# Graph attention with a residual norm: queries without an edge, their mean row, and two batches' halves in one tile

## The chip, the cores and the metric

The kernel runs on one core of a Trainium2 chip. The metric is the device time of one execution in microseconds (us). Five engines run side by side, each in the order of its own instructions: PE (matrix products), DVE (vector), ACT (scalar activations), POOL (which also issues all indirect DMAs) and SP (which issues plain DMAs). They wait for each other on semaphores.

## The reference

Inputs are x (16 batches of 1024 rows of 512), an adjacency matrix adj of 1024 x 1024 zeros and ones that all batches share, and four 512 x 512 weights with biases; all float32. There are 8 heads of 64.

```python
q = (x @ Wq + bq).reshape(b, n, H, HD)      # k and v alike
scores = jnp.einsum('bqhd,bkhd->bhqk', q, k) / jnp.sqrt(jnp.float32(HD))
scores = scores + (1.0 - adj)[None, None, :, :] * -1000000000.0
attn = jax.nn.softmax(scores, axis=-1)
out = jnp.einsum('bhqk,bkhd->bqhd', attn, v).reshape(b, n, d)
x = _layernorm(x + out @ Wo + bo, axis=-1)
```

The graph is sparse: of the 1024 queries 60 have no edge and 141 have one; the largest number is 66. A query without an edge has -1e9 added to every score. In float32 the scores vanish beside 1e9, all weights are equal, and its attention is the mean of all v. So every query without an edge of one batch has the same row of attention, and the same row after Wo. Only x differs from query to query.

## The kernel before

**Order by degree.** At the start the kernel sorts the queries by their number of edges (`ranks`, L404) and writes the sorted list to `order` in DRAM. A tile is 128 queries of like degree; there are NT = 8 per batch. `asked_row` holds the query numbers of each tile, and x, y and the output rows are gathered and stored by it, with indirect DMAs on POOL. `key_row` holds, for each tile and slot, the row of the key that each query attends to. Tile 0 holds the 64 lowest ranks (those without an edge, and here four with one) and ranks 192 to 255 (up to two edges). Tile 1 (ONE_KEY) holds ranks 64 to 191, which have one edge: their attention is just the v row of their key.

**Blocks.** A block is one slot of one tile: 128 queries, each with one key. `blocks` (L949) lists them over batches, tiles and slots: 34 per batch, 544 in all. `gather` (L958) fetches the k and v rows of a block (`kvg`, 128 rows of 4 KB, one indirect DMA on POOL) eight blocks ahead. DVE multiplies q with k (`products`, L1005) and adds up by head (`scores`, L1009); ACT takes exponentials (L1019); the v row is weighted by ACT in eight pieces (L1029) or by DVE (L1033); DVE adds the slots of one query (L1045). Slots beyond a query's degree carry a row number out of range and -1e9 in `absent`. The highest tiles have further blocks for spread-out edges, whose sums go through PE (L1054, L1055). `normalise` divides, `turn` transposes on PE (poT, L1088).

A query without an edge takes part in two blocks of tile 0: its key is row N of `kv_rows`, which holds zeros for k and the mean of v. `mean_pe` (L708) makes that mean for each batch.

**Fronts.** The other work of PE is the "fronts": x tiles are gathered (L817), transposed (pxT, L606), and multiplied into q (L639, all tiles but ONE_KEY) and into k and v by pairs of tiles (L763, a seven-product scheme). k and v rows of tile t go to DRAM by indirect DMA (L685), into one of ROWS = 3 rings `kv_rows[b % ROWS]`; q tiles go to `q_rows` by SP (L671) and come back by SP as `qt` (L972).

**Finish.** `finish` (L845) multiplies a turned tile with Wo (po, L639), adds x (`y`) and the bias, takes mean and variance (DVE L867, L868; ACT L875; a power on POOL L881), normalises on ACT (L889) and stores the rows with an indirect DMA on POOL (L893). While fronts last, bo_bc is added on DVE; afterwards a bf16 matmul (L940) puts it into the product.

**Spill and stored.** 20 tiles (SPILL) have their turned attention put to DRAM and are finished only after the last front. For the 42 tiles of STORED the front also writes the x tile to `residual`, from which SP loads y later; for all others y is gathered by POOL.

**The order.** Everything is laid out by hand in one loop over steps n, one per block. Each step issues its share of block work, deferred functions (`later`), and then units of fronts or finishes until a credit (`share`, costed by PRODUCT, SUM, TRANSPOSE) is spent. 39 steps of fronts alone lead in. From step (LATE + 1) * NBT on the share is set so that the fronts end 12 blocks before the last batch begins.

**The guard.** The equal weights hold only if |q||k| stays small. `squares` takes the norms of q in tile 0's edgeless rows (L649, sq_q) and of all k rows; `guard` (L1107) checks their product against LIMIT = 31, and if it fails a general path computes everything again.

Of the kernel before, what the change touches and what calls it, by code (L numbers as in the profile page):

```python
# [34 lines left out]
LONE, ONE_KEY, ONE_KEY_AT = 64, 1, (7, 4)  # L35
# [3 lines left out]
SPILL = (*range(36, 100, 4), *range(102, 106))  # L39
STORED = {*SPILL, *range(102, 128)}  # L40
# [14 lines left out]
BIAS_AT = -8  # L55
REST_FROM = {7: -24, 6: -9}
# [113 lines left out]
def kernel(  # L170
# [75 lines left out]
    with ExitStack() as main:  # L246
# [17 lines left out]
        place = one.tile([P, SPAN], F32, name="place")  # L264
# [18 lines left out]
        key_row = one.tile([P, NS + NK], I32, name="key_row")  # L283
        query_row, query_row0 = (one.tile([P, NS], I32, name=name) for name in ("query_row", "query_row0"))

        absent = one.tile([P, NK], F32, name="absent")
        check = one.tile([P, 2 * NT + 2], F32, name="check")

        lone = one.tile([P, 1], F32, name="lone")
        lone_norm = one.tile([P, B], F32, name="lone_norm")  # L290
# [4 lines left out]
        rank_row, asked_row = (one.tile([P, NT], I32, name=name) for name in ("rank_row", "asked_row"))  # L295
# [3 lines left out]
        kv_rows = [dram.tile([N + 1, 2 * D], F32, name=f"kv_rows_{i}") for i in range(ROWS)]  # L299
        q_rows = [dram.tile([N, D], F32, name=f"q_rows_{i}") for i in range(ROWS)]  # L300
        order = dram.tile([N, 2 + TOP], F32, name="order")
        kv_views = [dram_disjoint_views(rows, NT) for rows in kv_rows]
        order_views = dram_disjoint_views(order, NT)
        out_views = dram_disjoint_views(out, B * NT)
# [8 lines left out]
        def loads():  # L313
# [14 lines left out]
            for i in range(ROWS):  # L328
                nc.scalar.dma_start(kv_rows[i][N:N + 1, 0:D], zeros[0:1, 0:D])
                if i:  # L330
                    nc.scalar.dma_start(q_rows[i][ds(ONE_KEY * P, P), :], zeros[:, 0:D])
# [14 lines left out]
        def bias_setup():  # L346
# [6 lines left out]
            nc.vector.tensor_reduce(bk_norm, n4, axis=AX.X, op=OP.max)  # L353
            yield
# [48 lines left out]
        def ranks():  # L403
# [47 lines left out]
            nc.vector.tensor_copy(asked_row, ranked[:, :, 0])  # L451
# [19 lines left out]
            nc.vector.tensor_scalar(absent, absent, -NEG, None, op0=OP.mult)  # L471
# [4 lines left out]
            listed.update(SHORT)  # L476

# [12 lines left out]
        def edges(t):  # L490
# [34 lines left out]
            if J > SEGMENT:  # L525

                nc.vector.tensor_scalar(found[:, 0:J], kl[:, 0:J], 0.0, None, op0=OP.is_gt)
                nc.vector.tensor_reduce(st[:, 0:1], found[:, 0:J], axis=AX.X, op=OP.add)
                nc.vector.tensor_tensor(check[:, 2 * NT + 1:], ranked[:, t, 1:2], st[:, 0:1], op=OP.subtract)
# [56 lines left out]

        X, XT, SX, KV, VSUM, NRM, Y, OT, PS = {}, {}, {}, {}, {}, {}, {}, {}, {}
# [13 lines left out]
        def transpose_x(b, t):  # L601
            def pe():
# [5 lines left out]
                def out():  # L608
                    XT[b, t] = work.tile([P, D], F32, tag="xT", name=f"xT_{b}_{t}", bufs=4)
                    nc.scalar.copy(XT[b, t], p)  # L610
                    n = b * NT + t + 3
                    if b * NT + t in STORED:
# [33 lines left out]
        def squares(name, s, sums, scale=1.0):  # L646
            for h in range(NPAIR):
                sq = work.tile([P, P], F32, tag="sq", name=f"sq_{name}_{h}", bufs=2)
# [7 lines left out]
        def pair(b, j):  # L656
# [8 lines left out]
            def out_q(i, p):  # L665

                assert gathered[0] >= NBT * (b - ROWS + 1)
# [14 lines left out]
            def send(i):  # L682
                kv = KV[b, tt[i]]
                if b:
                    later(2, lambda: nc.gpsimd.indirect_dma_start(  # L685
                        out=kv_views[b % ROWS][tt[i]], out_offset=bass.IndirectOffsetOnAxis(ap=asked_row[:, tt[i]:tt[i] + 1], axis=0),
# [19 lines left out]
            def mean_pe():  # L706
# [3 lines left out]
                def out():  # L710
                    m = work.tile([1, D], F32, tag="q", name=f"mean_{b}", bufs=2)
                    nc.scalar.copy(m, p[0:1, :])  # L712
                    nc.sync.dma_start(kv_rows[b % ROWS][N:N + 1, D:], m)
# [3 lines left out]
                later(1, out)  # L717

# [6 lines left out]
            )  # L725
            n = b * NT + 2 * j + 2
# [94 lines left out]

        def load_y(b, t, k=None):
# [8 lines left out]
            if b * NT + t in STORED:  # L831
                nc.sync.dma_start(Y[b, t], residual[b * NT + t])
            else:
                gather_x(Y[b, t], b, t)
# [7 lines left out]
        def finish(b, t):  # L842


            biased = not fronts and now[0] < total  # L845

            if now[0] >= total:
                nc.vector.tensor_tensor(Y[b, t], Y[b, t], bo_bc, op=OP.add)

            fronts_then = bool(fronts)  # L850

            def out(p):
                OT.pop((b, t))
                y = Y[b, t]

                single = fronts or now[0] > total + 3
                if single:
                    st = small.tile([P, 5], F32, name="stats", bufs=6)
# [449 lines left out]
```

## Time and profile before

| | |
|---|---|
| median of 3 runs | 1929.36 us (1926.79 to 1929.45) |
| the profiled execution | 1928.59 us, of which its span (first to last instruction) is 1926.8 |
| mean granted clock of PE | 0.990 |
| DMA | 550.85 MB, mean 286 GB/s |
| indirect DMAs on POOL | kvg 544, stores 128, kv_rows 120, x 120, qg 96, y 86, v 16, qt 7 |

Busy times are unions of the records of one engine. A record of PE is longer than the pitch at which matmuls follow each other, since they overlap; the chain of waits gives the pitch. In a group of instructions the columns are line, engine and operation, what is written and read, the count, busy us and mean ns of one. In the timeline a bracket holds the idle time before an instruction and what released it.

By stage: until about 130 us the sort and the lead-in; from there 15 batches of about 111 us; the last front unit ends near 1776 us; then the last batch's blocks and 33 finishes, to the end.

### The profile page before, as it was taken

The page shows a single profiled execution, that of the slowest core. Times are in us where ns is not written, and L with a number is a line of the kernel's source. Part 1 is how long each engine was busy: PE and PEld are TensorE (multiplying, and loading weights), DVE is VectorE, ACT ScalarE, POOL GpSimd, SP SyncE. Part 2 cuts the span into 40 slices and gives each one's busy share as a digit, 9 for nine tenths or more (in the row PEclk, how much of TensorE's full clock was granted, in tenths as well). Part 3 has the DMA queues.
Part 4 walks back from the last instruction along what each step waited for, and adds up shares of the span by engine and source line. Part 5 has one row for each costly group of instructions (what it writes and reads, how often), then busy time and mean ns, then how long its engine had stood idle before and what let it go on. Part 6 is the DMA issues. An engine that isn't in the chain of part 4 may idle for free. (4 is left out here: it accounts for less than half of the span.)

```text
span 1926.8 us, 25037 instructions
## 1 busy us (share of the span) xinstructions
PE 1854.1 (96%) x5247; PEld 898.2 (47%) x5247; DVE 1724.8 (90%) x3494; ACT 1549.6 (80%) x6072; POOL 1368.9 (71%) x1262
## 2 busy tenths in 40 slices
PE   7989999999999999999999999999999989899996
PEld 3444454444544454444544454444544444444443
DVE  6888889899998999899998999899998989798885
ACT  3638779878888888889897888888897988788785
POOL 1336667878787777878778788877787777665785
PEclk9999999999999999999999999999999999999998
DMA  7357788888889898898989898988899898888994
GB/s 273 122 179 243 247 276 265 291 273 290 301 273 314 273 305 299 296 315 296 315 267 323 286 326 288 316 294 297 310 316 325 281 334 301 296 287 283 365 328 167
DMA packets 189313, 550.85 MB, mean 286 GB/s; under 512 B 31359, under 2 KB 31371, under 8 KB 189150
## 3 DMA queue, kind: packets, MB, share of 16 engines
q0 software_dynamic: 133584, 447.59, 69.1%
q1 hardware_dynamic: 52672, 96.04, 13.6%
q10 hardware_dynamic: 2894, 5.52, 0.9%
q14 instruction: 119, 0.97, 0.2%
q8 instruction: 44, 0.72, 0.2%
HBM read 426.56 MB, written 147.18 MB: 298 GB/s over the span
## 5 line engine op out<-in xcount | busy, mean ns | idle before, releaser
L1029 ACT ACTIVATE pv<-kvg,pv 128x64 f32<-128x64 f32 x3544 | 892.1, 338 | 0.0
L984 POOL DMA_INDIRECT kvg<-kv_rows,key_row x544 | 624.6, 1148 | 240.8 <-issue 84.8
L639 PE MATMUL pq<-wq,xT 128*128 128x512 f32 x904 | 422.5, 598 | 0.9 <-ACT mean L712 0.9
L639 PE MATMUL po<-wo,oT 128*128 128x512 f32 x864 | 401.2, 597 | 1.0 <-ACT oT L1092 0.9
L1009 DVE TENSOR_REDUCE s<-qk 128x8 f32<-128x512 f32 x544 | 369.5, 679 | 7.5
L1005 DVE TENSOR_TENSOR qk<-qt,kvg 128x512 f32<-128x512 f32 x448 | 306.5, 684 | 37.4 <-DMA kvg<-kv_rows,key_row 37.0
L639 PEld LDWEIGHTS pq<-wq,xT 128*128 128x128 f32 x904 | 169.1, 192 | 193.4 <-issue 179.4
L639 PEld LDWEIGHTS po<-wo,oT 128*128 128x128 f32 x864 | 162.9, 191 | 182.9 <-issue 169.4
L763 PE MATMUL x<-b,xT 128*128 128x512 f32 x504 | 238.1, 595 | 0.0
L763 PE MATMUL pp<-t,s 128*128 128x512 f32 x504 | 237.4, 593 | 0.0
L1045 DVE TENSOR_TENSOR pv<-pv,pv 128x520 f32<-128x520 f32 x336 | 232.7, 692 | 0.9 <-ACT pv L1029 0.9
L1019 ACT ACTIVATE pv<-s,absent 128x8 f32<-128x8 f32 x448 | 130.2, 292 | 84.7 <-DVE s L1009 79.3
L817 POOL DMA_INDIRECT x<-in_x_dram,asked_row x120 | 134.2, 1118 | 76.7 <-PE pxT L606 34.6
L893 POOL DMA_INDIRECT out_dram<-y,asked_row x128 | 146.8, 1147 | 40.8 <-issue 19.3
L685 POOL DMA_INDIRECT kv_rows<-kv,asked_row x120 | 135.9, 1132 | 33.8 <-issue 22.9
L649 ACT ACTIVATE sq_k<-kv 128x128 f32<-128x128 f32 x512 | 150.6, 299 | 7.8 <-DVE kv L786 7.8
L763 PEld LDWEIGHTS x<-b,xT 128*128 128x128 f32 x504 | 95.2, 191 | 114.9 <-issue 109.2
L763 PEld LDWEIGHTS pp<-t,s 128*128 128x128 f32 x504 | 94.3, 190 | 110.6 <-issue 102.6
L954 POOL DMA_INDIRECT qg<-q_rows,query_row x96 | 108.1, 1126 | 31.2 <-issue 25.7
L763 PE MATMUL z<-b,s 128*128 128x512 f32 x252 | 118.8, 594 | 1.0 <-DVE kv L791 0.9
L763 PE MATMUL z<-t,s 128*128 128x512 f32 x252 | 119.6, 597 | 0.0
L763 PE MATMUL pp<-t,xT 128*128 128x512 f32 x252 | 118.4, 592 | 0.0
(208 smaller groups left out, 2666.3 us busy)
## 6 DMA issues: line engine op xcount, KB each, us to landing
q_rows<-q SPq DMA_DIRECT2D x113, 256.0 KB
qt<-q_rows SPq DMA_DIRECT2D x105, 256.0 KB
residual<-x SPq DMA_DIRECT2D x42, 256.0 KB
y<-residual SPq DMA_DIRECT2D x42, 256.0 KB
kvg<-kv_rows,key_row POOLq DMA_INDIRECT x544, 5.9
spill<-oT SPq DMA_DIRECT2D x20, 256.0 KB
oTs<-spill SPq DMA_DIRECT2D x20, 256.0 KB
adj<-in_adj_dram POOLq DMA_DIRECT2D x8, 512.0 KB, 13.4
```

The lines of the kernel that those rows point to most:

```text
L639: nc.tensor.matmul(p, lhs(c), w[:, c, :], start=(c == 0), stop=(c == NPAIR - 1))
L649: nc.scalar.activation(sq, s[:, ts(h, P)], AF.Square, scale=scale, accum_out=sums[:, h:h + 1])
L685: later(2, lambda: nc.gpsimd.indirect_dma_start(out=kv_views[b % ROWS][tt[i]], out_offset=bass.IndirectOffsetOnAxis(ap=asked_row[:, tt[i]: ...
L763: nc.tensor.matmul(R[bank], l[:, ts(c, P)], right[:, c, :], start=(first and c == 0), stop=(c == 1), skip_group_check=True,)
L817: nc.gpsimd.indirect_dma_start(out=y, out_offset=None, in_=x_rows, in_offset=bass.IndirectOffsetOnAxis(ap=asked_row[:, t:t + 1], axis=0), ...
L893: nc.gpsimd.indirect_dma_start(out=out_rows[b, t], out_offset=bass.IndirectOffsetOnAxis(ap=asked_row[:, t:t + 1], axis=0), in_=y, in_offse ...
L984: nc.gpsimd.indirect_dma_start(out=KG[n], out_offset=None, in_=kv_rows[b % ROWS], in_offset=bass.IndirectOffsetOnAxis(ap=key_row[:, g:g + ...
L1005: nc.vector.tensor_tensor(QK[n], q, KG[n][:, 0:D], op=OP.mult)
L1009: nc.vector.tensor_reduce(S[n], QK.pop(n).rearrange("p (h d) -> p h d", d=HD), axis=AX.X, op=OP.add)
L1019: nc.scalar.activation(PV[n][:, D:], S.pop(n), AF.Exp, bias=bias)
L1029: nc.scalar.activation(pv[:, ts(h, HD)], v[:, ds(D + h * HD, HD)], AF.Copy, scale=pv[:, D + h:D + h + 1])
L1045: nc.vector.tensor_tensor(PV[b, t], PV[b, t], pv, op=OP.add)
```

## The change

For batches 2 to 15 (PAIRED_FROM = 2), taken in pairs of an even and an odd batch:

- **The one-edge tile moves down by eight ranks.** It becomes ranks 56 to 183 (column A of a new list `others`), so that its first row is a query without an edge, whose key row is the mean. After Wo its row 0 is the attention output of every edgeless query; `keep_mean` copies it and SP writes it to `mean_rows`.
- **The 56 edgeless queries of two batches form one tile of 112 rows (L).** `load_lone` broadcasts the two mean rows over 56 rows each (SP), gathers y, and four steps later `complete` (the second half of the old `finish`) adds, normalises and stores. It has no q, no blocks, no turn and no Wo product.
- **The two-edge halves (ranks 192 to 255) of two batches form one merged tile 0 (M)** of the odd batch. Its q comes from a product on `BOTH`, into which ACT copies the right halves of both batches' transposed x. Its two kvg gathers are made in halves of 64 rows, one from each batch. The even batch has no tile 0: 32 blocks, no q product, turn or finish.
- **The eight one-edge queries left over per batch (ranks 184 to 191)** have their v rows gathered by two 8-row DMAs per pair into `more_rows`; all 112 form one tile MORE, turned and finished in the last batch.
- **The guard** bounds the q norms of the edgeless queries from a bf16 product of the upper halves of the float32 words (`lone_product`: four matmuls, eight squares per pair), plus a term from the norms of x (sq_x) and Wq.
- kv_rows gets four rings for three; STORED loses tiles 0 and 1 of the last batches (36 tiles for 42); SPILL holds other tiles, 20 as before. In the last batch the one-edge tile is turned earlier (ONE_KEY_LAST).

```diff
-LONE, ONE_KEY, ONE_KEY_AT = 64, 1, (7, 4)
+LONE, ONE_KEY, ONE_KEY_AT, ONE_KEY_LAST = 64, 1, (7, 4), (3, 0)
+PAIRED_FROM, SPARED = 2, 56
+LONE_TILE, MORE_TILE, MORE_AT = 8, 9, (5, 0)
-SPILL = (*range(36, 100, 4), *range(102, 106))
-STORED = {*SPILL, *range(102, 128)}
+SPILL = (*(8 * b + t for b in range(4, 12) for t in (3, 6)), 102, 103, 106, 107)
+STORED = {*SPILL, *(i for i in range(102, 128) if i % 8 > 1)}
...
+        def more_ranks():
+            A, M, L, X = range(4)
+            for col, at, lo, hi in ((A, 0, SPARED, SPARED + P), (M, 0, LONE + P, 2 * P), (M, LONE, LONE + P, 2 * P), (L, 0, 0, SPARED), (L, SPARED, 0, SPARED)):
+                nc.sync.dma_start(others[at:at + hi - lo, col, :], order[lo:hi, :])
+            spare, n = LONE - SPARED, B - PAIRED_FROM
+            lo = SPARED + P
+            for i in range(n):
+                nc.sync.dma_start(others[spare * i:spare * (i + 1), X, :], order[lo:lo + spare, :])
...
+            for h in range(HEADS):
...
+                nc.scalar.activation(sq, W["q"][:, :, ts(h, HD)], AF.Square, accum_out=wq_norm[:, h:h + 1])
...
                     nc.scalar.copy(XT[b, t], p)
+                    if t == 0 and b >= PAIRED_FROM:
+                        if not merged(b):
+                            BOTH[b // 2] = work.tile([P, 2, NPAIR, P], F32, tag="place", name=f"both_{b}", bufs=1)
+                        nc.scalar.copy(
+                            BOTH[b // 2].rearrange("p w c (h n) -> p h c w n", h=2)[:, b % 2],
+                            p.rearrange("p (c w n) -> p c w n", c=NPAIR, w=2),
+                        )
+                        sq = work.tile([P, D], F32, tag="ysq", name=f"sq_x_{b}", bufs=1)
+                        nc.scalar.activation(sq[0:LONE, :], xs[0:LONE, :], AF.Square, accum_out=x_norm[0:LONE, b:b + 1])
...
+                    for c in range(NPAIR):
+                        nc.tensor.matmul(
+                            p, high(both[:, 0, c, :]), high(W["q"][:, c, :]), start=(c == 0), stop=(c == NPAIR - 1)
+                        )
...
+            if j == 0 and b >= PAIRED_FROM:
+                q0 = []
+                if merged(b):
+                    q0 = product(f"pq_{b}_0", lambda c: BOTH[b // 2][:, 1, c, :], W["q"], lambda p: out_q(0, p))
+                    q0 += lone_product()
...
+        def load_lone(b):
+            Y[b, "mean"] = work.tile([P, D], F32, tag="y", name=f"means_{b}", bufs=Y_BUFS)
+            for i in range(2):
+                nc.sync.dma_start(
+                    Y[b, "mean"][SPARED * i:SPARED * (i + 1), :], mean_rows[b - 1 + i:b + i, :].to_broadcast([SPARED, D])
+                )
+            load_y(b, LONE_TILE)
+            later(4, lambda: complete(b, LONE_TILE, Y.pop((b, "mean")), True))
+
+        def keep_mean(b, p):
+            m = work.tile([1, D], F32, tag="q", name=f"out_mean_{b}", bufs=2)
+            nc.scalar.copy(m, p[0:1, :])
+            nc.sync.dma_start(mean_rows[b:b + 1, :], m)
+            if merged(b):
+                later(2, lambda: lone_tiles.append(b))
...
-        blocks = [(b, t, i) for b in range(B) for t in range(NT) if t != ONE_KEY for i in range(OWN[t] + BLOCKS[t])]
+        blocks = [(b, t, i) for b in range(B) for t in tiles_of(b) if t != ONE_KEY for i in range(OWN[t] + BLOCKS[t])]
...
+            if merged(b) and (t, i) == (0, 0):
+                n2, g2 = LONE - SPARED, NS + NK + 3
+                more = work.tile([P, D], F32, tag="qt", name=f"more_{b}", bufs=Q_BUFS)
+                for h in range(2):
+                    nc.gpsimd.indirect_dma_start(
+                        out=more[h * n2:(h + 1) * n2, :], out_offset=None, in_=kv_of(b - 1 + h),
+                        in_offset=bass.IndirectOffsetOnAxis(ap=key_row[0:n2, g2:g2 + 1], axis=0), element_offset=D,
+                    )
...
-            nc.gpsimd.indirect_dma_start(
-                out=KG[n], out_offset=None, in_=kv_rows[b % ROWS],
-                in_offset=bass.IndirectOffsetOnAxis(ap=key_row[:, g:g + 1], axis=0),
-                bounds_check=N, oob_is_err=False,
-            )
+            halves = 1 + (merged(b) and t == 0)
+            for h in range(halves):
+                at = slice(h * P // halves, (h + 1) * P // halves)
+                nc.gpsimd.indirect_dma_start(
+                    out=KG[n][at, :], out_offset=None, in_=kv_of(b + 1 + h - halves),
+                    in_offset=bass.IndirectOffsetOnAxis(ap=key_row[0:P // halves, g:g + 1], axis=0),
+                    bounds_check=N, oob_is_err=False,
+                )
```

## The prediction

> **What bounds the kernel now.** I read part 1 of the page first, then the windows of the middle, the chain that ended last, and the waits and timeline of single engines.
>
> ```profile
> PE 1854.1 (96%) x5247; PEld 898.2 (47%) x5247; DVE 1724.8 (90%) x3494; ACT 1549.6 (80%) x6072; POOL 1368.9 (71%) x1262
> ```
>
> PE leads, and POOL looks as if it had 29% to spare. By windows (columns: PE, PEld, DVE, ACT, POOL busy us, clock, DMA share, GB/s):
>
> ```profile
> 600.00:800.00 200.00, 196.90 (x567) 95.96 (x566) 187.89 (x370) 170.95 (x684) 155.65 (x142) 1.00 0.87 297
> 800.00:1000.00 200.00, 197.56 (x569) 96.25 (x568) 188.44 (x368) 173.83 (x704) 151.74 (x140) 1.00 0.88 298
> 1000.00:1200.00 200.00, 196.35 (x563) 96.83 (x562) 187.76 (x368) 169.05 (x685) 157.25 (x143) 0.99 0.91 307
> 1200.00:1400.00 200.00, 197.04 (x566) 96.02 (x565) 188.34 (x367) 172.41 (x698) 155.11 (x139) 1.00 0.88 303
> 1400.00:1600.00 200.00, 190.46 (x548) 93.13 (x547) 183.02 (x357) 171.24 (x690) 149.64 (x138) 0.99 0.91 313
> ```
>
> The middle is uniform: PE 978 of 1000 us (97.8%), DVE 935, ACT 857, POOL 769 with 702 instructions. The chain of waits is PE back to back until 1765 and again from 1776 to 1860:
>
> ```profile
> 1820.86 1.72 PE po L639 x4
> 1822.58 0.44 PE poT L1088 x4
> 1823.01 1.72 PE po L639 x4
> 1824.95 3.43 PE po L639 x8
> 1828.60 3.43 PE po L639 x8
> ```
>
> A product of four float32 matmuls (eight records) thus costs PE 3.43 us, four transposes 0.44. The 0.22 between 1823.01 + 1.72 and 1824.95 is the one bf16 bias matmul.
>
> The timeline of POOL shows what its share hides:
>
> ```profile
> 941.95 1.02 POOL L984 DMA_INDIRECT kvg<-kv_rows,key_row  x1 [0.31 <-ACT pv L1019]
> 943.27 0.97 POOL L817 DMA_INDIRECT x<-in_x_dram,asked_row  x1 [0.31 <-issue]
> 944.54 1.25 POOL L984 DMA_INDIRECT kvg<-kv_rows,key_row  x1 [0.30 <-ACT pv L1029]
> 946.09 0.95 POOL L817 DMA_INDIRECT x<-in_x_dram,asked_row  x1 [0.30 <-PE poT L1088]
> 947.35 1.00 POOL L984 DMA_INDIRECT kvg<-kv_rows,key_row  x1 [0.30 <-issue]
> ```
>
> Every indirect DMA is preceded by 0.30 us whichever releaser is named: dispatch, not waiting. Of the 702 instructions about 630 are DMAs (eight powers per batch are not); 630 x 0.30, a little less behind a power, is about 181 us. So POOL is occupied for 769 + 181 = 950 of 1000 us. It is the second bound, 3% behind PE. The waits of 400 to 1600 (us, times, longest; POOL's first, then DVE's) agree: 43 times make 15.5, so most are the 0.30 again.
>
> ```profile
> POOL kvg L984 <- DVE pv L1033: 21.0, 13, 3.1
> ...
> POOL kvg L984 <- ACT pv L1019: 15.5, 43, 2.7
> ...
> POOL x L817 <- PE pxT L606: 5.1, 3, 2.6
> ```
>
> ```profile
> DVE qk L1005 <- DMA kvg<-kv_rows,key_row: 35.5, 26, 4.5
> ```
>
> **What the Trainium skill says.** "TensorE: Matmul & The Clock Gate", section "Back-to-back issue gap": an isolated 512-column bf16 matmul follows its predecessor after about 216 ns; the 0.22 us of the bias matmul agrees. "DMA: Bandwidth & Descriptors", section "Anatomy of one DMA — SWDGE (gpsimd) path": such a DMA has a fixed cost that does not shrink with its size, and descriptor generation is "small, variable". Here an indirect DMA takes POOL 1143 ns with 40-byte rows (order), 1118 with 2 KB (x) and 1148 with 4 KB (kvg), all of 128 rows; no fewer rows are seen, and the page prices none. The same page, "Issuing engines are not separate DMA queues": DMAs of SP, ACT and POOL share the 16 engines; the DMA share of 0.87 to 0.91 is all of them together. For a price: "ScalarE: Activation LUTs", section "What ACT_TABLE_LOAD costs", gives 186 ns + 0.833 ns per column with immediate scale and bias, 293 for 128 columns; sq_k L649 shows 299.
>
> **The change, part by part.** The first and last sq_q of L649 (126.7 and 1792.0) stand 15 batches apart: 111 us each, 222 per pair. Of a pair's 222 us PE fills 217.0, POOL 210.8, DVE 207.5, ACT 190. Seven pairs, batches 2 to 15, change.
>
> PE, per pair: tile 0 of the even batch goes, with its q product (3.43), its transposes (0.44) and its output product (3.43): -7.30. Added are four bf16 matmuls of phat at 0.22 = 0.88; their operands skip every second half-word, which the trace doesn't show, so up to 0.43 each, the pitch of a float32 record: 0.88 to 1.72, I take 0.88. Net -6.4 to -5.6. Once, at the end, the MORE tile: 0.44 + 3.43 + 0.22 = +4.1. In all 7 x -6.4 + 4.1 = -41 us.
>
> DVE, per pair, at the 0.60 pitch of the chain: two qk, two s, one pv addition, one o, one q: -4.2, and small ones (rden, two lone_norm, less one lone_hat) about -0.4: -4.6. The L tile is finished like the tile that went (L867, L868, stats), so nothing is saved there. DVE's 207.5 becomes 202.9.
>
> ACT, per pair: two rounds of eight weightings at 2.0 us (the timeline's "x8") and exponentials, eight sq_q with read-outs (0.39 + 0.19, overlapping) and an oT copy: about -9. Added: two BOTH copies (0.57, as L610; its strided write is unmeasured, 0.57 to 1.2), two sq_x (about 0.8 with read-out), eight phat squares of 64 columns (an estimate of 239 ns from that ScalarE page, with read-outs about 2.4 to 3.4), two mean copies (0.56): +6 to +8. ACT stays near 188; below PE and POOL, it costs nothing.
>
> POOL, per pair: two whole kvg gathers of the even batch go, two of the odd batch become four halves, two small gathers "more" are added. Four DMAs of 1.3 us become six. If row count has no weight, +2.6 us; if a half costs 0.75 us and a small one 0.55 (the direct DMAs of L407 and L408 show 0.55 to 0.585), plus 0.30 each: 4.2 + 1.7 against 5.2, +0.7; slightly below nothing if halves cost half. Bounds -0.5 to +2.6, I take +1.0: 211.8. STORED shrinks from 42 tiles to 36, so seven more y gathers come on POOL, nearly all after batch 13.
>
> So a pair's loads become POOL 211.8, PE 210.6, DVE 202.9. Today a pair takes 5 us more than its fullest engine. With two engines level I allow 0.7 more: 211.8 + 5 + 0.7 = 217.5, a saving of 4.5 per pair, 31.5 in all. The other 1.9 of PE's 6.4 is what comes late next, POOL's dispatch.
>
> The tail, 1776 to the end. There POOL runs gather on store with 0.30 between, and PE is full until 1860. POOL gets four y gathers (A, merged and L tile of 15, MORE; before, all y of the tail came by SP from STORED), two stores and two extra halves: 8 x 1.3 = 10.4 us; PE gets MORE's 4.1. POOL has some 4 us of true waits before 1895. Bounds +4 to +10.5, I take +7.
>
> The lead-in: 19 small SP loads of order, zeros for one more q tile and for more_rows on ACT's queue, some twenty small DVE instructions (0.15 each) and eight squares of wq (about 0.5 each on an ACT that is busy 20 of 50 us from 100 to 150): 0 to +3, I take +1. SP is waiting for q for 1161 us of the run and has room for them, for the mean rows and their broadcasts. The step queue gives these broadcasts four steps, 13 us, against 4 to 6 us that DMAs take to land here. Other moves (ONE_KEY_LAST, guard later, four kv buffers in DRAM for three) issue nothing more.
>
> Sum: -31.5 + 7 + 1 = -23.5. The profiled execution took 1928.59 (span 1926.8, 1.8 around it); 1905.1, and as the median of the three runs is 0.8 above it, 1905.
>
> **The rivals.**
> 1. PE alone decides. For it: it leads every window and the chain. Then -41 holds whole: 1888. Against it: POOL's 950 of 1000.
> 2. The saving is nearly eaten: halves and small gathers cost a full 1.3 us, the pair saves only 222 - (213.4 + 5 + 1.4) = 2.2, 15 in all, and the tail takes 10.5 and the lead-in 1 to 3: 1925, 1917 to 1928. For it: 2 KB and 4 KB rows cost POOL the same.
> 3. Slower: a new wait in POOL's queue. load_x gathers into the buffer that pxT has read; with the change sq_x on ACT reads it too, 14 times, behind a copy and BOTH (0.57 each) and, if unlucky, a round of weightings (2.0). POOL then stands, and the kvg gathers queued behind it stand, for which DVE waits (35.5 us today). Beyond 23.5 / 14 = 1.7 us a time it turns the result; at 2.5 us it costs 35: 1940. For it: the same gather already waits for pxT (34.6 us, 9 times over the run). Against it: POOL mostly arrives late and finds ACT done, and it is eight blocks ahead.
> 4. The change falls back to the general path. From the inputs: 60 queries have no edge, so rank 56 has none; the new bound is 15.1 (largest key norm) x (1.36 + 0.0158 x 0.125 x 24.7 x 8.05) = 26.4, under the limit of 31. Excluded.
>
> **How the numbers follow.** My forecast (1905, own range 1894 to 1917) has 0.45, PE alone (1888) 0.23, nearly eaten 0.14, slower (1940) 0.18. A change of 0.2%, 4 us, is what this measurement can tell from none; half of the second rival lies within it. Faster 0.75, same 0.07, slower 0.18. The range from 1884, the strided bf16 and a POOL that gains included, to 1928 leaves the slower case and the lowest few per cent out.
>
> **What would show it.** Right: pq records fall by 56 to 848, po (both forms) by 56 and then up 8 to 976; PE's total by about 41; POOL's dispatch-counted load near 96% in the middle while PE's share there falls below 97.5%; a pair takes about 217.5 us; from the end of the last front unit to the end some 7 us more. The 64-row gathers settle POOL's term: near 0.75 us is my case, 1.1 is the second rival. PE's middle share still at 97.8% and pairs at 215.5 would be the first rival; x L817 waiting for ACT sq_x by over 1.7 us a time the third. A lone tile's y waiting on DVE for its mean broadcast would be a wait that I hold to be hidden.

## The result, and the profile after

| | before | after |
|---|---|---|
| median | 1929.4 us (1926.79 to 1930.34) | 1955.77 us (1945.1 to 1960.38) |
| ratio to before | | 1.0131, 95% interval 1.0089 to 1.0173 |
| profiled execution, its span | 1928.59, 1926.8 | 1954.99, 1953.0 |
| mean granted clock of PE | 0.990 | 0.984 |

The changed kernel is slower by 26 us where 24 fewer were forecast. Part 1 of the page:

```profile
PE 1830.3 (94%) x5148; PEld 880.7 (45%) x5148; DVE 1700.1 (87%) x3468; ACT 1534.0 (79%) x6015; POOL 1379.7 (71%) x1289
```

The work did go: PE has 99 instructions fewer, DVE 26, ACT 57. But all three are idle more, and POOL is the one engine with more to do (27 instructions, 11 us). The same windows of the middle (columns: PE, PEld, DVE, ACT, POOL busy us, clock, DMA share, GB/s):

```profile
600.00:800.00 200.00, 190.69 (x553) 92.28 (x552) 182.10 (x360) 168.45 (x678) 151.41 (x142) 1.00 0.86 292
800.00:1000.00 200.00, 185.48 (x520) 90.00 (x519) 176.52 (x342) 160.31 (x642) 150.10 (x138) 0.97 0.87 288
1000.00:1200.00 200.00, 186.86 (x528) 90.81 (x528) 175.03 (x340) 159.24 (x647) 152.21 (x137) 0.98 0.85 287
1200.00:1400.00 200.00, 188.18 (x538) 92.14 (x537) 177.31 (x346) 166.34 (x675) 153.19 (x139) 0.97 0.86 290
1400.00:1600.00 200.00, 189.06 (x539) 91.66 (x538) 180.39 (x352) 167.16 (x673) 153.69 (x143) 0.99 0.87 301
```

PE fills 940 of 1000 us where it filled 978, DVE 891 for 935. POOL is unmoved: 761 for 769, with 699 instructions for 702. That is the first sign: the engine that kept its load is the one that kept its rate.

By stage, from the first exponential of one batch to that of another (added up from the traces, us):

```
                  before   after
lead-in            133.5   136.4
batches 0 and 1    243.4   245.9
batches 2 to 13   1300.9  1313.0    (a pair: 216.8, 218.8)
batch 14           115.5   116.0
tail               133.4   141.7
```

So the middle did not save 4.5 us a pair but lost 2.0. Of POOL it has 152.2 instructions a pair for 151.0. Where does PE stand idle? The waits of 400 to 1600 (us, times, longest), POOL's, DVE's and PE's, with PE's of the kernel before last:

```profile
POOL kvg L1178 <- ACT pv L1214: 20.7, 45, 1.9
...
POOL kvg L1178 <- DVE pv L1228: 14.5, 7, 3.8
...
POOL x L948 <- ACT sq_x L708: 6.1, 4, 3.4
```

```profile
DVE qk L1199 <- DMA kvg<-kv_rows,key_row: 66.4, 39, 6.0
...
DVE qk L1199 <- issue: 9.6, 2, 5.4
```

```profile
PE sum L1249 <- DVE pv L1228: 29.6, 13, 5.0
```

```profile
PE sum L1054 <- DVE pv L1033: 11.4, 7, 3.8
```

DVE's wait for gathered k and v rows grew from 35.5 to 66.4 us (and 9.6 more are put down to "issue", where two half-gathers have to land); PE's wait behind it, for the weighted rows of the spread blocks, grew from 11.4 to 29.6. POOL is held little: its waits on DVE's pv are 14.5 us, 21.0 before, and most other entries are the 0.30 of dispatch. What it waits beyond those is 10.5 us a pair, 8.8 before; that is a small share, but a large part of the 2.0 us by which a pair grew, and the experiments come back to it. One start of an odd batch shows how. The timeline of POOL, the bracket giving the idle time before an instruction and what released it:

```profile
916.21 1.45 POOL L1072 DMA_INDIRECT out_dram<-y,asked_row  x1 [0.19 <-DMA kvg<-kv_rows,key_row]
917.96 1.01 POOL L1072 DMA_INDIRECT out_dram<-y,asked_row  x1 [0.30 <-issue]
919.27 0.98 POOL L948 DMA_INDIRECT x<-in_x_dram,asked_row  x1 [0.30 <-issue]
920.56 0.96 POOL L948 DMA_INDIRECT x<-in_x_dram,asked_row  x1 [0.30 <-issue]
921.83 0.89 POOL L1150 DMA_INDIRECT more<-kv_rows,key_row  x1 [0.31 <-DMA out_dram<-y,asked_row]
923.02 0.86 POOL L1150 DMA_INDIRECT more<-kv_rows,key_row  x1 [0.31 <-issue]
924.19 1.05 POOL L1178 DMA_INDIRECT kvg<-kv_rows,key_row  x1 [0.30 <-ACT pv L1214]
925.55 0.95 POOL L1178 DMA_INDIRECT kvg<-kv_rows,key_row  x1 [0.31 <-DMA x<-in_x_dram,asked_row]
926.80 0.94 POOL L1178 DMA_INDIRECT kvg<-kv_rows,key_row  x1 [0.30 <-issue]
928.05 0.93 POOL L1178 DMA_INDIRECT kvg<-kv_rows,key_row  x1 [0.30 <-issue]
```

Not one real wait: every bracket is the dispatch of 0.30 us (0.31 at most). The two more-gathers and four halves fill 921.83 to 928.98, where two whole gathers would have been. DVE and PE in the same stretch:

```profile
925.04 0.68 DVE L910 TENSOR_TENSOR w<-pp,e 128x512 f32<-128x512 f32 x1
929.92 0.69 DVE L1199 TENSOR_TENSOR qk<-qt,kvg 128x512 f32<-128x512 f32 x1 [4.19 <-issue]
```

```profile
924.00 2.74 PE L736 MATMUL po<-wo,oT 128*128 128x512 f32 x6
931.27 1.22 PE L1249 MATMUL sum<-pv,sums 128*128 128x256 f32 x2 [4.53 <-DVE pv L1228]
932.28 1.09 PE L1250 MATMUL sum<-pv,sums 128*128 128x264 f32 x2
933.16 1.91 PE L736 MATMUL pq<-wq,xT 128*128 128x512 f32 x2
...
936.60 1.07 PE L736 MATMUL pq<-wq,xT 128*128 128x512 f32 x2
...
939.23 0.59 PE L1249 MATMUL sum<-pv,sums 128*128 128x256 f32 x2
```

The second half of the first block was issued at 925.55. DVE had finished everything else at 925.72, so it stood for 4.19 us until this half had landed and its product could begin at 929.92; PE stood for 4.53. PE then paid again: the same two sum matmuls take 1.22 at 931 and 0.59 at 939, two pq matmuls 1.91 at 933 and 1.07 at 936.60. The Trainium skill, "TensorE: Matmul & The Clock Gate", section "What's actually happening", says that the clock gate halves PE's clock after an idle window of about 3.4 us and opens again after as long a busy one. The trace agrees on the halving: after this gap of 4.53 us the granted clock of 931 to 937 us is 0.53, and the records are about twice as long. They stay so for 5.3 us, from 931.27 to 936.60, longer than one such window.

Over the starts of batches 3, 5, ... 15, DVE's idle time in the first eight products (gaps of over half a microsecond) sums to 52.5 us, where it was 16.1 before.

### The profile page after: what moved, and what is told of

Read it like the earlier page. It is cut to its first block, busy times and chain, and to the rows that moved or that the text cites. A ratio compares the mean times of both kernels' runs of the same rounds, so it can differ in the third digit from the quotient of the medians.

```text
span 1953.0 us, 24856 instructions
## 1 busy us (share of the span) xinstructions
PE 1830.3 (94%) x5148; PEld 880.7 (45%) x5148; DVE 1700.1 (87%) x3468; ACT 1534.0 (79%) x6015; POOL 1379.7 (71%) x1289
## 3 DMA queue, kind: packets, MB, share of 16 engines
q1 hardware_dynamic: 50972, 91.37, 13.2%
## 4 chain that ended last, share of the span: by engine, by line
PE 41%; DVE 24%; DMA 11%; ACT 9%; issue 7%; POOL 3%; POOLq 0%; DVEq 0%; ACTq 0%; SPq 0%
PE po L736 10%; PE pq L736 9%; DMA kvg<-kv_rows,key_row 8%; PE pp L894 7%; PE x L894 6%; DVE qk L1199 5%; ACT pv L1224 5%; PE z L894 5%; DVE s L1203 4%; DVE pv L1240 3%; PE poT L1284 2%; PE pxT L694 1%; DVE q L767 1%; DMA out_dram<-y,asked_row 1%; DVE y L1046 1%
## 5 line engine op out<-in xcount | busy, mean ns | idle before, releaser
L1224 ACT ACTIVATE pv<-kvg,pv 128x64 f32<-128x64 f32 x3432 | 864.3, 339 | 0.0
L1178 POOL DMA_INDIRECT kvg<-kv_rows,key_row x544 | 610.9, 1123 | 242.1 <-issue 81.7
L736 PE MATMUL po<-wo,oT 128*128 128x512 f32 x816 | 383.1, 600 | 1.0 <-ACT oT L1288 0.9
L736 PE MATMUL pq<-wq,xT 128*128 128x512 f32 x792 | 373.5, 604 | 2.1 <-DVE q L767 1.5
L1199 DVE TENSOR_TENSOR qk<-qt,kvg 128x512 f32<-128x512 f32 x434 | 297.0, 684 | 81.0 <-DMA kvg<-kv_rows,key_row 63.8
L1203 DVE TENSOR_REDUCE s<-qk 128x8 f32<-128x512 f32 x530 | 360.5, 680 | 7.9 <-DVE qk L1199 0.5
L736 PEld LDWEIGHTS po<-wo,oT 128*128 128x128 f32 x816 | 153.8, 193 | 168.8 <-issue 154.4
L736 PEld LDWEIGHTS pq<-wq,xT 128*128 128x128 f32 x792 | 150.7, 194 | 170.4 <-issue 154.3
L746 ACT ACTIVATE sq_k<-kv 128x128 bf16<-128x128 f32 x512 | 150.9, 301 | 8.0 <-DVE kv L917 8.0
L976 POOL DMA_INDIRECT y<-in_x_dram,asked_row x93 | 103.4, 1112 | 27.6 <-issue 25.6
```

The source lines that it names most:

```text
L736: nc.tensor.matmul(p, lhs(c), w[:, c, :], start=(c == 0), stop=(c == NPAIR - 1))
L746: nc.scalar.activation(sq, s[:, ts(h, P)], AF.Square, scale=scale, accum_out=sums[:, h:h + 1])
L1178: nc.gpsimd.indirect_dma_start(out=KG[n][at, :], out_offset=None, in_=kv_of(b + 1 + h - halves), in_offset=bass.IndirectOffsetOnAxis(ap=ke ...
L1199: nc.vector.tensor_tensor(QK[n], q, KG[n][:, 0:D], op=OP.mult)
L1203: nc.vector.tensor_reduce(S[n], QK.pop(n).rearrange("p (h d) -> p h d", d=HD), axis=AX.X, op=OP.add)
L1224: nc.scalar.activation(pv[:, ts(h, HD)], v[:, ds(D + h * HD, HD)], AF.Copy, scale=pv[:, D + h:D + h + 1])
```

## The experiments

Two theories came out of this. In the expectations' letters, A: POOL's number of instructions sets an even pace, wherever they stand. F: it is their place, six DMAs at the head of each odd batch, right behind the burst of the last tile's spread blocks with two DMAs each. Three rivals are set against them. B: PE sets the pace, and the change lost its gain elsewhere. C: the wait for sq_x in POOL's queue ate the gain. D: the change's order of work costs it, not POOL's load.

**PE's time taken away, and POOL's added, in the kernel before.** b_less_pe leaves 49 matmuls out of the q and output products of the even batches; b_more_pool adds 28 gathers of eight rows.

```diff
+        FEW = {}
+        for even in range(2, B, 2):
+            FEW.update({f"pq_{even}_0": 1, f"po_{even}_2": 1, f"po_{even}_6": 3})
...
-                nc.tensor.matmul(p, lhs(c), w[:, c, :], start=(c == 0), stop=(c == NPAIR - 1))
+                used = FEW.get(name, NPAIR)
+                if c < used:
+                    nc.tensor.matmul(p, lhs(c), w[:, c, :], start=(c == 0), stop=(c == used - 1))
```

```diff
+            if b >= 2 and b % 2 and (t, i) in ((0, 0), (5, 0)):
+                g = NS + own[ONE_KEY]
+                for h in range(2):
+                    more = work.tile([8, D // 8], F32, tag=f"more{h}", name=f"more_{b}_{t}_{h}", bufs=1)
+                    nc.gpsimd.indirect_dma_start(
+                        out=more, out_offset=None, in_=kv_rows[(b - 1 + h) % ROWS],
+                        in_offset=bass.IndirectOffsetOnAxis(ap=key_row[0:8, g:g + 1], axis=0), element_offset=D,
+                    )
```

> The kernel before with PE work left out alone: for each even batch from 2 on, three matmuls of the q product of tile 0, three of the Wo product of tile 2 and one of the Wo product of tile 6 are missing (7 x 0.86 us a pair, 42 us in all; those outputs are partial sums). Every other engine has the same instructions. Theory A (POOL's indirect DMAs at about 1.0 us and 0.3 of dispatch set the pace, PE is just behind): no more than 10 us faster, 1919 to 1930. Theory B (PE sets the pace and the change lost its gain elsewhere): 35 to 42 us faster, 1888 to 1894.

> The kernel before with four more indirect gathers of 8 rows (256 bytes each) per pair of batches from 2 on, 28 in all, into buffers that nobody reads. Theory A: each takes POOL 0.9 + 0.3 us, 34 us in all, and with POOL occupied 95% of the time at least half of it reaches the end: 17 to 34 us slower, 1946 to 1963. Theory B: POOL has room and nothing waits for these gathers: at most 5 us slower.

The kernel before took 1927.68 us on this chip. b_less_pe: 1925.12, ratio 0.9983 (0.9966 to 1.0). Its windows of the middle:

```profile
sum 1000.00, PE 956.62 PEld 466.10 DVE 927.59 ACT 850.59 POOL 768.30; mean PE 191.32 PEld 93.22 DVE 185.52 ACT 170.12 POOL 153.66
```

PE's load fell from 978 to 957 of 1000 us, and POOL's stayed at 768: most of the work left out turned into idle time. 42 us of PE were worth 2.6, with an interval that reaches to nothing. b_more_pool: 1940.08, ratio 1.0074 (1.0051 to 1.0098): 12.4 us for 28 DMAs, 0.44 each, about a third of what each occupies POOL for (0.91 and the 0.30). That lies between the forecasts of A and B. So POOL's DMAs count before the change too, but there is still some slack between them.

**The added DMAs, and sq_x, taken from the changed kernel.** a_less_pool leaves the 14 more-gathers out and fetches each merged block with one gather of 128 rows, from one batch only; POOL has 28 DMAs fewer, and SP loses the seven small stores of these rows as well. a_no_sqx leaves out the 14 squares of x.

```diff
-            halves = 1 + (merged(b) and t == 0)
+            halves = 1
...
-                for h in range(2):
-                    nc.gpsimd.indirect_dma_start(
-                        out=more[h * n2:(h + 1) * n2, :], out_offset=None, in_=kv_of(b - 1 + h),
-                        in_offset=bass.IndirectOffsetOnAxis(ap=key_row[0:n2, g2:g2 + 1], axis=0), element_offset=D,
-                    )
```

```diff
-                        sq = work.tile([P, D], F32, tag="ysq", name=f"sq_x_{b}", bufs=1)
-                        nc.scalar.activation(sq[0:LONE, :], xs[0:LONE, :], AF.Square, accum_out=x_norm[0:LONE, b:b + 1])
```

> The changed kernel without the two small gathers per pair (the MORE tile is made of zeros) and with one gather of 128 rows of the odd batch in place of the two halves, so the even batch's half of the merged tile uses the wrong batch's rows: four POOL DMAs fewer per pair, 28 in all, nothing else. Theory A: 20 to 36 us faster than the changed kernel, 1920 to 1936. Theory B: within 5 us of it, 1951 to 1960.

> The changed kernel without the 14 squares of x (sq_x; the guard's term for the norm of x is left at zero), which hold the x buffer that POOL's next gather writes. Theory C (this wait in POOL's queue ate the gain): at least 25 us faster than the changed kernel, below 1931. Theory A: the trace shows POOL waiting 7.4 us for it in 6 of 14 places, so 0 to 7 us faster, 1948 to 1956.

a_less_pool: 1930.02, ratio 1.0024 (1.001 to 1.0037); a_no_sqx: 1947.75, ratio 1.0116 (1.0086 to 1.0147). The waits of a_less_pool, 400 to 1600, DVE's and PE's:

```profile
DVE qk L1192 <- DMA kvg<-kv_rows,key_row: 50.1, 33, 4.2
```

```profile
PE sum L1242 <- DVE pv L1221: 14.7, 9, 4.3
```

Four DMAs fewer per pair give back 21 to 26 us (1.0131, and 1.0160 in a later run, to 1.0024, times 1928): nearly all that the change lost. The order of work is still the changed kernel's, so this speaks against D as the main cause. In the profiled execution, which was 4.7 us shorter than the median, a pair falls to 214.1 us, 2.7 below the kernel before, and PE's wait for the spread blocks to half. The wait for sq_x (C) is small: removing it gave 3 to 8 us, with intervals that overlap or just touch.

What POOL does in a pair, added up from the traces for batches 2 to 13 (us; dispatch is up to 0.31 before each instruction):

```
                  before   b_more_pool   a_less_pool   after
busy               166.5         169.1         162.8   166.4
dispatch            41.4          42.6          40.6    41.8
further waits        8.8           6.6          10.6    10.5
a pair             216.8         218.1         214.1   218.8
```

From a_less_pool to the changed kernel, the four DMAs add 4.8 us of busy time and dispatch, the waits stay, and the pair grows by 4.7: there they pass on in full. In the kernel before, four more add 3.8, but the waits shrink by 2.2, and the pair grows by 1.3. And a_less_pool has 4.5 us less of POOL's own work than the kernel before and yet saves only 2.7, since POOL's waits are 1.8 longer. So the changed order has a cost too, which no run isolates.

**POOL relieved of its other instructions.** In b_no_power and a_no_power DVE does a multiplication in place of POOL's powers; b_pair_power and a_pair_power take one power for two tiles where one was taken for each.

```diff
-                nc.gpsimd.tensor_tensor(st[:, 3:4], st[:, 2:3], neg_half[0:n, :], op=OP.pow)
+                nc.vector.tensor_scalar(st[:, 3:4], st[:, 2:3], -0.5, None, op0=OP.mult)
```

```diff
-            single = fronts or now[0] > total + 3 or n < P
+            single = now[0] > total + 3 or n < P
```

> The kernel before without the 112 powers on POOL: the inverse root of the variance is left out, DVE writes a scaled variance in its place (output not normalised in size). POOL loses 16 instructions of about 0.7 us a pair of 217. Theory A: POOL no longer leads, PE's 97.2% of a pair then sets the floor at 211 us: 10 to 40 us faster, 1888 to 1918. Theory B: nothing but shorter finish chains: within 10 us.

> The changed kernel with the same left out. Theory A: with POOL out of the way the PE work that the change removed shows at last: PE's floor is 94.4% of 218.8 = 206.5 us a pair, the run at least 45 us faster than the changed kernel and 5 to 30 us faster than the kernel before without powers: 1870 to 1905. Theory D (the change's order of work, not POOL's load, costs the gain): it stays 15 us or more slower than the kernel before without powers.

> The kernel before with the powers joined in the same way. Theory A: POOL is relieved but PE is 3% behind: 3 to 20 us faster, 1908 to 1926. Theory B: no change, or slower because y buffers are held longer.

> The changed kernel, with the powers of two tiles joined into one POOL instruction during the fronts too, as both kernels do after them (the rows then wait up to six steps longer for their store). Same output. POOL loses about 7 instructions of 0.9 us with dispatch a pair. Theory A: 15 to 35 us faster than the changed kernel, 1921 to 1941. Theory D: within 8 us of it.

Ratios: b_no_power 1.0096 (1.0059 to 1.0133), a_no_power 1.027 (1.0234 to 1.0307), b_pair_power 1.0024 (0.9988 to 1.006), a_pair_power 1.0245 (1.0172 to 1.0318). None gained, against theory A as it stands in its simplest form. And a_no_power stays 33 us above b_no_power, which is what theory D forecast for it; the changed kernel itself has no reading on this chip, so how much of the 33 the missing powers gave or took is not known. D as the main cause has a_less_pool against it. Also, this chip was another one: the kernel before took 1964 us on it, and in both no_power traces DVE stands for 68 and 94 us, ACT for 72 and 97, in gaps of over 1 us that no event explains (1 us for ACT in the profiles of before and after; for DVE none before, 20 after, at the half-gathers). POOL's own real waits tripled, from 9 to 28 us a pair in b_no_power, much of it for buffers of kvg. Part of that may be the chip's doing: b_v1 below, with all its powers, shows 14 on a chip of that kind. POOL had time to spare there and the kernel was no faster, so its load does not set the pace by itself. More these four can't tell.

**The six DMAs moved.** a_m_later takes the merged tile after tile 3 in the odd batches; nothing is added or removed.

```diff
-            return [t for t in range(NT) if t or b < PAIRED_FROM or merged(b)]
+            if merged(b):
+                return [2, 3, 0, 1, *range(4, NT)]
+            return [t for t in range(NT) if t or b < PAIRED_FROM]
```

> The changed kernel with one thing moved: in odd batches the merged tile 0 is taken after tile 3 and not first, so that its two more-gathers and four half-gathers no longer follow at once on tile 7's spread blocks, which issue two indirect DMAs each. Every count of instructions on every engine stays. Theory F (the six DMAs come where POOL is already latest; DVE then waits at the head of each odd batch, 52 us of gaps in seven starts against 16 before, and PE and ACT behind it): 20 to 36 us come back, 1920 to 1936 where the changed kernel takes 1956; DVE's gaps in the first eight products of the odd batches fall from 52 to under 25 us. Theory A (POOL's number of instructions sets an even pace, wherever they stand): within 5 us of the changed kernel.

It fell on a third chip where the kernel before took 1992 us (DVE and ACT with 80 and 112 us of unexplained gaps): ratio 1.0058 (1.0028 to 1.0088). Repeated, as a_m_later_q on a fourth (1994 us) and at last on one where the kernel before took 1927.88, beside the changed kernel itself:

> The kernel of a_m_later once more, beside a_stored on one chip, since the chip of that run had stalls of its own (the kernel before took 1992 us there, and the idle time of DVE and ACT that no releaser explains came to 80 and 112 us against 20 and 1 in the changed kernel's profile). Theory F: ratio 0.995 to 1.003 (20 to 36 us back). Theory A: 1.011 to 1.015. Half of it (8 to 14 us, ratio 1.005 to 1.009), as the disturbed run had it: both causes.

> The changed kernel as it is, as the measure for the runs whose chip stalled on its own: its ratio to the kernel before on this chip. If 1.011 to 1.015 as first measured, then a_m_later (1.0058) and a_m_later_q (1.0068) did give back 8 to 14 us by place alone, and a_stored (0.9991) 24 to 30 us by number. If about 1.006, then the place of the six DMAs gave nothing (theory F falls) and a_stored 14 us.

> The kernel with the merged tile after tile 3, once more and now beside the changed kernel itself on one chip. Theory F: 20 to 36 us below a_again. Theory A: within 5 us of it. Both: 8 to 14 us below it.

a_m_later_q: ratio 1.0068 (1.004 to 1.0095). a_again: 1958.05, ratio 1.0160 (1.0146 to 1.0174). a_m_later_r: 1949.95, ratio 1.0103 (1.0082 to 1.0123): 8.1 us below a_again, intervals apart, at the lower edge of what was expected if both causes hold. In its timeline of POOL the six stand with other work before and after them, but at the same pitch:

```profile
935.73 0.90 POOL L1152 DMA_INDIRECT more<-kv_rows,key_row  x1 [0.30 <-issue]
936.94 0.87 POOL L1152 DMA_INDIRECT more<-kv_rows,key_row  x1 [0.31 <-issue]
938.11 1.48 POOL L1180 DMA_INDIRECT kvg<-kv_rows,key_row  x1 [0.30 <-DMA kvg<-kv_rows,key_row]
```

```profile
DVE qk L1201 <- DMA kvg<-kv_rows,key_row: 63.7, 44, 4.8
...
DVE qk L1201 <- issue: 4.1, 3, 2.6
```

```profile
PE sum L1251 <- DVE pv L1230: 23.3, 13, 4.6
```

With the entries put down to issue, DVE waits 67.8 us in this window, where it was 76.0 in the changed kernel's first profile and 74.7 in a_again, and in shorter pieces (the longest 4.8 for 6.0); PE waits less too (23.3, for 29.6 and 32.5). DVE's gaps in the first eight products of the odd batches fall to 38 us (56 in a_again), not below 25 as F expected. POOL's waits beyond dispatch fall from 10.5 to 6.4 us a pair, while the same DMAs occupy it for 2.8 longer. So place is real and is 8 us, about a third of what F expected. The rest of the four DMAs' 21 to 26 us, 13 to 18, is put down to their number by subtraction; that would be 0.5 to 0.6 us for each, near the 0.44 of b_more_pool.

**DMAs given to another queue.** a_stored and b_stored take 24 y gathers, evenly spread, from POOL; SP writes and loads those x tiles. Everything is computed.

```diff
-STORED = {*SPILL, *(i for i in range(102, 128) if i % 8 > 1)}
+STORED = {*SPILL, *(i for i in range(102, 128) if i % 8 > 1), *(8 * b + t for b in range(2, 14) for t in (2, 5))}
```

> The changed kernel with 24 of POOL's y gathers handed to SP: tiles 2 and 5 of batches 2 to 13 join STORED, so the front writes their x tile to residual and SP loads y from there. Nothing else changes; everything is computed. Theory A (POOL's number of instructions sets an even pace of 1.2 to 1.4 us each): 24 x 0.9 to 1.4 = 20 to 34 us below the changed kernel, so a ratio to the kernel before of 0.995 to 1.003. Theory F (only the six DMAs at the head of the odd batches count): within 6 us of the changed kernel, ratio 1.010 to 1.013.

> The kernel before with the same 24 y gathers handed from POOL to SP. If POOL sets the pace before the change too: 12 us (0.5 each, as much as 28 added gathers cost there) to 30 us below it, ratio 0.985 to 0.994. If PE sets it there, as predicted: at most 4 us, ratio 0.998 to 1.0.

(The edit is a_stored's; b_stored adds the same tiles to the list before.) a_stored: ratio 0.9991 (0.9966 to 1.0015), below a_m_later_q on the same chip (1.0068), with the six DMAs left in their place. b_stored: ratio 0.9953 (0.9934 to 0.9971), about 9 us for 24 DMAs, between its two forecasts. Against the changed kernel's 1.0131 to 1.0160, measured elsewhere, a_stored gives 1.4 to 1.7%, 27 to 33 us; the chip had unexplained gaps of its own (DVE and ACT about 90 us each in a_stored), so that size is no more than likely. The sign is A's. b_stored moves 556.6 MB where the kernel before moves 550.9 and is faster all the same, which speaks against the amount of data as the pace.

**Moves that don't add up.** a_mended adds to a_m_later an earlier more_ranks and a later x gather; a_mended_v1 and b_v1 move the v gather of the one-edge tile from tile 7 to 5 (shown for b_v1); a_stored_mended is a_stored with a_mended's moves.

```diff
-MORE_RANKS_AT = -12
+MORE_RANKS_AT = -24
...
+                    elif t == 0 and b >= PAIRED_FROM:
+                        later(1, lambda: load_x(n // NT, n % NT))
```

```diff
-LONE, ONE_KEY, ONE_KEY_AT = 64, 1, (7, 4)
+LONE, ONE_KEY, ONE_KEY_AT = 64, 1, (5, 4)
```

> a_m_later with two further moves: more_ranks starts 24 steps ahead of the first block and not 12, so that the first gather that shares its list does not wait for it (9.2 us in the lead-in of the changed kernel), and the x gather that reuses the buffer which sq_x reads is issued one step later. Theory F: 6 to 12 us below a_m_later, 1910 to 1928, with lead-in and batch 0 together back from 273 to about 266 us. If the lead-in's 9 us come from the extra work there and not from that wait: within 3 us of a_m_later.

> a_mended with the gather of the one-edge tile's v rows moved from tile 7 (the POOL burst at the end of a batch) to tile 5. Theory F: a further 0 to 8 us, since that burst shrinks by one DMA in every batch. Theory A: within 3 us of a_mended.

> The kernel before with the same move of the v gather to tile 5. Theory F: 0 to 6 us below the kernel before (1922 to 1928), since the first products of a batch wait little there (36 us of gaps over fourteen starts). Theory A: no change.

> a_stored with the three moves of a_mended (merged tile after tile 3 in the odd batches, more_ranks 24 steps ahead, the x gather behind sq_x one step later). If both causes hold and add up: 12 to 25 us below a_stored, ratio 0.985 to 0.994. If a POOL with room makes the place of the six DMAs indifferent: only the lead-in's and batch 0's 3 to 8 us.

Ratios: a_mended 1.002 (0.9987 to 1.0053), a_mended_v1 1.0105 (1.0071 to 1.014), b_v1 0.9906 (0.9881 to 0.9932), a_stored_mended 1.0075 (1.0048 to 1.0101). a_mended lies 7.6 us below a_m_later, as F expected, but the intervals overlap, and the lead-in and batch 0 take 275 us, no less than the changed kernel's 273: POOL's first kvg gather no longer waits 9.2 us for the list, but 8.4 for the mean row, as it did before the change (8.0).

a_stored_mended goes against both causes. It is a_stored with the six DMAs moved, and is 13 us slower on the same chip, intervals apart. It is also a_m_later_q with 24 DMAs fewer on POOL, and is no faster (1.0075 and 1.0068). No run explains this.

The two v1 kernels have short waits of DVE for kvg (12 and 8 us in 400 to 1600), yet one is the slowest of the four on its chip and the other the fastest; DVE and ACT have 86 and 132 us of unexplained gaps in a_mended_v1 and 48 and 65 in b_v1. Where these gaps come from, and why they differ between kernels, is open; while they do, sizes of about 1% from these chips aren't settled. b_stored and b_v1 were faster than the kernel before there, and neither was measured on a chip without such gaps.

## Why the prediction was wrong, by its steps

- **PE, -41 us; DVE, -4.6 a pair.** Right as work: records of pq fell to 848 and of po to 976, as forecast, and DVE's load of a pair fell by 5.1 us; phat's strided matmuls take hardly longer than the bias matmul's (387 ns and 379), so the lower price was the right one. PE's busy time fell by only 24 us, though, since part of the records ran at half clock: 0.6% less granted clock over 1953 us is, as an estimate, 12 us.

```profile
L828 PE MATMUL phat<-wq,both x28: 385/387/390, 311.6 to 1678.9; 128*128 128x512 bf16 x28
```

- **"Today a pair takes 5 us more than its fullest engine": the step that failed.** It takes a load off the fullest engine and keeps the rest constant, so PE's work becomes time. b_less_pe shows that it doesn't. By the prediction's own sum, its 6 us a pair off PE turn 222 into 211.0 + 5 + 0.7 = 216.7, 37 us in all; measured are 2.6. A share of 97.8% did not mean that PE set the pace. As the waits have it, PE was fed by a chain of POOL's gathers, DVE's products and ACT's weights about as long, and its units filled what that chain left; that chain was not taken apart link by link. The 222 us were off too, since they are an average over 15 batches: a pair of batches 2 to 13 takes 216.8. But PE's share of that is 212.0, so the 5 us between them were there; that they would stay when the load fell was the mistake.
- **POOL, +1.0 a pair.** The six DMAs were mis-sized, near the wrong end of their bounds. The small gathers, and all gathers of kvg with the 28 halves among them, have these durations (ns: least, median, most):

```profile
L1150 POOL DMA_INDIRECT more<-kv_rows,key_row x14: 855/900/1418, 478.7 to 1797.7; - x14
```

```profile
L1178 POOL DMA_INDIRECT kvg<-kv_rows,key_row x544: 920/1020/2153, 115.4 to 1905.7; - x182
```

Eight rows cost 0.90 us, a half 0.95 in the median of 28, where I took 0.55 and 0.75 from direct DMAs and a guess. Six DMAs at about 1.25 with dispatch against four at 1.3: +2.3, close to rival 2's +2.6. The Trainium skill ("DMA: Bandwidth & Descriptors", section "Anatomy of one DMA — SWDGE (gpsimd) path") says of this path's setup and completion that they do not shrink with the size. Of POOL's share in it the page says less; the trace shows that it hardly shrinks either, 0.90 us for eight rows and 1.02 for 128, and I had quoted the sentence without following it. In these kernels the price is nearly all per DMA, little per row. POOL's whole load of a pair rose by 0.3 us only, because other instructions took less time; of the 2.0 us that a pair lost, the other 1.7 are longer waits of POOL.

- **That POOL's term would enter only as a load.** With even rival 2's price the sum gave 1925. What the sum had no place for is when the six come: after the burst, so that the first block's gather was issued when DVE had already run out of work, and landed 4.3 us later. Then come DVE's gap, PE's, and half a clock. Place is the 8 us of a_m_later_r; number is what is left of a_less_pool's 21 to 26.
- **Rival 3, the wait for sq_x.** The mechanism is in the waits, 6.1 us in four times, longest 3.4, and gave 3 to 8 us when removed. It was priced at 35 and did not decide.
- **The tail, +7.** Too small. From the first exponential of batch 15 it is +8.3 (+11.6 in a_again). But the prediction counted from the end of the last front unit (the product of `mean_pe`, at 1776.1 before and 1789.1 after), and from there to the end it is +13.2 (+16.6 in a_again), beyond its bound of 10.5. MORE's tile has its part in it: in the chain that ended last, PE's products run on to 1876, with the turn of MORE at 1867:

```profile
1867.29 1.02 PE poT L1284 x8
1868.32 1.72 PE po L736 x4
1870.25 3.43 PE po L736 x8
1873.90 1.73 PE po L736 x4
```

- **The lead-in, +1.** Too small: lead-in and batches 0 and 1 take 5.4 us more. Not through the wait for the list, as a_mended showed; the earlier work there was not taken apart further.
- **The mean's broadcast.** Right: no wait of DVE on it in the trace.

How much of the middle is number and how much place is known only as these two sizes, 21 to 26 us for both and 8 for the move; the kernel with fewer DMAs and the six moved has no reading from an undisturbed chip, and a_stored_mended's speaks against a plain sum, so whether they add up stays open.

The sum as measured, by stage: lead-in and batches 0 and 1 +5.4, batches 2 to 13 +12.1, batch 14 +0.5, batch 15 and the end +8.3: +26. In the prediction's terms: up to the end of the last front unit +13.0, where -31.5 and +1 were forecast, and from there +13.2 for +7. (1929.36 less 23.5 is 1905.9, so the forecast itself should have read 1906; nothing hangs on it.)

## What to carry to other kernels

An engine at 98% is the bound only if taking work off it gives time; a run that leaves some of it out settles that before the real change is written. Where one engine issues all gathers, as POOL does here, count its DMAs, not bytes or rows: splitting one gather into two cost nearly a whole one. Look where in the queue new DMAs fall: moving six of them from behind a burst gave back 8 us with not one of them removed.

## What was not expected of the hardware

An indirect DMA of eight rows occupies POOL for 0.90 us, one of 64 rows for 0.95, one of 128 rows of 4 KB for 1.02 in the median. After a gap of 4.53 us PE's matmuls took about twice as long for 5.3 us, so a stall of DVE costs PE more than itself. And the same kernel took 1928, 1964, 1992 and 1994 us on different chips, the slower ones with tens of microseconds of gaps of DVE and ACT that no event in the trace explains.
